# Norms' small steps and half of the state sums on GpSimd, softplus and an attention reciprocal kept in PSUM

## The chip, the cores and the metric

The kernel runs on one core of a Trainium2 chip. The metric is the time of one execution on the device in microseconds (us); lower is better. The core's engines work side by side, each through its own queue in order: PE (TensorE, matmuls), DVE (VectorE), ACT (ScalarE), POOL (GpSimd), and SP, which only issues transfers here. SBUF is the on-chip memory that all of them use; PSUM holds what PE writes, and DVE and ACT read and write it too.

## The reference, cut to what matters

Four sequences of 1024 tokens of 256 values pass four sub-layers, each as x = x + layernorm(f(layernorm(x))):

```python
x = x + _layernorm(_L0_attn_ref(_layernorm(x), ...))  # 4 layers of linear attention and MLP
x = x + _layernorm(_L0_ffn_ref(_layernorm(x), ...))   # a gated low-rank layer
x = x + _layernorm(_L1_attn_ref(_layernorm(x), ...))  # a state space model (SSM)
x = x + _layernorm(_L1_ffn_ref(_layernorm(x), ...))   # 8 experts, one per token, at most 320 each
```

A norm is (x - mean) / sqrt(var + 1e-5). In an attention layer, with q and k passed through elu + 1, the output is divided by a sum:

```python
z = 1.0 / (jnp.einsum('blhd,bhd->blh', qp, ksum) + EPS_ATTN)
return jnp.einsum('blhd,bhmd,blh->blhm', qp, kv, z)
```

In the SSM, delta is a softplus, and 16 states per channel run along the sequence and are summed into the output:

```python
delta = jax.nn.softplus(dt @ W_dt + b_dt)
h = h * exp(delta * A) + (delta * u) * B_t        # for each of 16 states
y = sum over the 16 states of h * C_t
```

All is computed in float32.

## The kernel before, in words

**Blocks and units.** The tokens are worked in 8 blocks of 512 (TB), two per sequence, each as 4 tiles of 128 tokens. A unit is one attention layer of one block; two sequences go through the layers in turns. The loop at the end of `layers` calls the parts of several units in each step, so that one unit's matmuls stand beside another's norms: `a_norm` (L654, first norm), `a_turn`, `a_query`, `a_keys`, `a_sums`, `a_fold`, `b_heads` (L777, the division), `b_out` (L790, output and second norm), `f_up` and `f_down` (the MLP), and after the last layer `c_norm` to `c_norm3` and `c_gate` (the low-rank layer). Between the parts, `pump` draws pieces of the SSM and the experts from a generator, `stream`. For each block it runs `front(j)` (L1045: projections, convolution, softplus), `scan(j)` (L1159: the states), `back(j)` (output projection and norms) and `route(j)` (choice of expert). The experts run beside the last two blocks' scans. So attention and SSM overlap once the first sequence has left the attention layers, and the SSM of the last sequence comes after all of them.

**The order of the work.** No instruction goes out as it is written in the code. `Program.record` (L191) notes each with its operands and with what it will cost by a table of costs, a fixed part and a part per column for each operation of each engine (GPSIMD_NS at L144 is POOL's). `Program.order` (L289) then goes through all of them as a list scheduler. It takes whichever operation can start first by these costs, and gives it a buffer of its pool at that moment. The result is one fixed queue for each engine. So an operation that is cheaper, dearer, or on another engine moves the others too. The profile shows a helper's line, L203, for nearly every operation, so groups are told apart by the names of their tiles.

**A norm.** `ln_stats` (L451) takes mean and variance on DVE (`st`, `mv`). `ln_rsqrt` (L438) takes a first estimate `r` of the reciprocal root on ACT (Ln, then Exp), and improves it in three small DVE operations on 4 columns: `t<-r`, `t<-mv,t` (or `t<-var,t`, `t<-pp,t`), `rs<-t,r`. `norm_on_act` (L470) and `norm_by_act` (L498) then form `nb` on DVE in one more, and ACT applies both to four tiles of 256 columns. 145 norms run: 105 by `norm_on_act`, 32 by `norm_by_act`, and 8 of the experts, which call `ln_rsqrt` alone.

**The division.** In `b_heads`, two 512-column sums per unit are turned into z = exp(-ln(sum + eps)) on ACT, in an SBUF tile of pool `qe`, and DVE multiplies the queries `qT` by it. PE's results go to four PSUM banks of pool `ps_mm` (names `mm`), each given back after its last reader.

**Softplus.** For each of the four 128-channel groups of a block, `front` takes |x| and relu(x) from PSUM on ACT. It forms log(1 + e) of e = exp(-|x|) with a correction (`v1`: one DVE step and two on POOL), adds the relu (`e`, tile `t<-sg,qe` in the profile), multiplies by the input (`t<-xc,t`), and stores both halves of `du` to memory.

**The scan.** A block has 4 groups of 128 channels. Each is worked in 2 rounds r of 4 quarters q, a quarter being 16 channels by 8 states on the 128 partitions, and twice for the two halves of the 16 states (k = 0 and 1): 64 steps a block, 512 in all. Each step is: POOL multiplies `dbu` = (delta u) B, ACT takes `h` = exp(delta A) into PSUM, DVE runs the recurrence over 512 positions in place in `h`, keeps the last column (in a sequence's first half), and multiplies `hc` = h C. PE sums the states of `hc` into `y` by a matmul with a 0/1 matrix; the four quarters of a round go out together. A round's sums are held back and issued during the next one. Buffers: 3 of `dbu`, 2 PSUM banks of `h`, 8 of `hc`, one bank of `y`. The kernel also leaves on POOL the bias additions `X<-X,ro`, scale and residual of other norms (`tok<-tok,...`), a gate product (`ys`), and the scatter transfers of the experts.

Of the kernel before, what the change touches and what calls it, by code (L numbers as in the profile page):

```python
# [9 lines left out]
F32 = mybir.dt.float32  # L10
I32 = mybir.dt.int32
AF = mybir.ActivationFunctionType
# [128 lines left out]
    "reciprocal": (147, 5.84),  # L141
    "memset": (60, 0.83),
}
GPSIMD_NS = {"tensor_tensor": (190, 2.14), "tensor_copy": (200, 0.6), "memset": (100, 0.8)}  # L144
SCALAR_NS = {"activation": (215, 0.85), "copy": (150, 0.85)}

OVERLAP = {"vector": 84, "scalar": 99, "gpsimd": 42}
# [239 lines left out]
def sandwich_kernel(ctx: ExitStack, tc: tile.TileContext, io: dict):  # L387
# [49 lines left out]

    def ln_rsqrt(var, n, scale=1.0):  # L438

        r = small.tile([P, n], F32, tag="r", name="r")  # L440
        nc.scalar.activation(r, var, AF.Ln, bias=eps, scale=scale)
        nc.scalar.activation(r, r, AF.Exp, scale=-0.5)

        t = small.tile([P, n], F32, tag="t", name="t")
        nc.vector.scalar_tensor_tensor(t, r, -0.5 * scale, r, ALU.mult, ALU.mult)
        nc.vector.scalar_tensor_tensor(t, var, LN_EPS / scale, t, ALU.add, ALU.mult)
        rs = small.tile([P, n], F32, tag="rs", name="rs")
        nc.vector.scalar_tensor_tensor(rs, t, 1.5, r, ALU.add, ALU.mult)
        return rs

    def ln_stats(src, n=NT):  # L451
# [18 lines left out]
    def norm_on_act(dst, src):  # L470

        n = src.shape[1]
        mv, rs = ln_stats(src, n)
        nb = small.tile([P, n], F32, tag="nb", name="nb")
        nc.vector.scalar_tensor_tensor(nb, mv[:, :, 0], -1.0, rs, ALU.mult, ALU.mult)
        for i in range(n):
            nc.scalar.activation(
                dst[:, i, :], src[:, i, :], AF.Identity, bias=nb[:, i : i + 1], scale=rs[:, i : i + 1]
            )
# [18 lines left out]
    def norm_by_act(dst, src):  # L498

        sums = small.tile([P, NT], F32, tag="sums", name="sums")  # L500
        for i in range(NT):
            nc.scalar.activation(
                dst[:, i, :], src[:, i, :], AF.Copy, scale=-1.0 / D, accum_out=sums[:, i : i + 1]
            )
        var = small.tile([P, NT], F32, tag="var", name="var")
        for i in range(NT):
            nc.scalar.activation(
                dst[:, i, :],
                src[:, i, :],
                AF.Square,  # L510
                bias=sums[:, i : i + 1],
                accum_out=var[:, i : i + 1],
            )
        rs = ln_rsqrt(var, NT, 1.0 / D)
        nb = small.tile([P, NT], F32, tag="nb", name="nb")
        nc.vector.tensor_tensor(nb, sums, rs, ALU.mult)
        for i in range(NT):
            nc.scalar.activation(
                dst[:, i, :], src[:, i, :], AF.Identity, bias=nb[:, i : i + 1], scale=rs[:, i : i + 1]
            )  # L520
# [23 lines left out]
    def layers(ctx: ExitStack):  # L544
# [232 lines left out]
        def b_heads(u):  # L777
            j = units[u][2]
            qT, den = S[u]["qT"], S[u].pop("den")
            nc.gpsimd.tensor_tensor(X[j], X[j], over_tiles(weight(u)["ro"][:, 0, :]), ALU.add)  # L780
            for c in range(NC_D):
                ps = mm([P, TB], "psa")
                nc.tensor.matmul(ps, den[:, c, :], qT[:, c, :], start=True, stop=True)

                z = apool.tile([P, TB], F32, tag="qe", name="z")
                nc.scalar.activation(z, ps, AF.Ln, bias=attn_eps)
                nc.scalar.activation(z, z, AF.Exp, scale=-1.0)
                nc.vector.tensor_tensor(qT[:, c, :], qT[:, c, :], z, ALU.mult)

        def b_out(u):  # L790
            j = units[u][2]
# [253 lines left out]
        def front(j):  # L1045
# [89 lines left out]
            for db in range(NDB):  # L1135
                ps = mm([P, TB], "psdt")
                o = db * 32
                nc.tensor.matmul(
                    ps, m["w_dt"][o : o + DT_RANK, :], dbc[o : o + DT_RANK, :], start=True, stop=True
                )  # L1140
                bdt = mcol[:, db, M_BDT : M_BDT + 1]
                du = fpool.tile([P, 2, TB], F32, tag="t4", name="du", bufs=3)
                e, lv = du[:, 0, :], du[:, 1, :]
                v1 = fpool.tile([P, TB], F32, tag="sg", name="v1", bufs=2)
                nc.scalar.activation(e, ps, AF.Abs, bias=bdt)
                r = apool.tile([P, TB], F32, tag="qe", name="over")
                nc.scalar.activation(r, ps, AF.Relu, bias=bdt)
                nc.scalar.activation(e, e, AF.Exp, scale=-1.0)
                nc.scalar.activation(lv, e, AF.Ln, bias=1.0)
                nc.vector.tensor_scalar(v1, e, 1.0, -1.0, ALU.add, ALU.add)  # L1150
                nc.gpsimd.tensor_tensor(v1, e, v1, ALU.subtract)
                nc.gpsimd.tensor_tensor(v1, v1, lv, ALU.add)
                nc.vector.tensor_tensor(e, v1, r, ALU.add)
                nc.vector.tensor_tensor(lv, xc[:, db, :], e, ALU.mult)
                store(dud[j][db], du)
                yield 2
                flush()

        def scan(j):  # L1159
# [12 lines left out]
            for db in range(NDB):  # L1172
                y = ps_y.tile([P, TB], F32, tag="y", name="y")

                def sums(tiles, r, k):
                    for q in range(4):
                        nc.tensor.matmul(
                            y[q * 32 : (q + 1) * 32, :],
                            m["gsum"][:, r, :],
                            tiles[q, k],  # L1180
                            start=r == 0 and k == 0,
                            stop=r == GQ - 1 and k == NSH - 1,
                        )

                late = []
                for r in range(GQ):
                    if r == GQ // 2:
                        xl = fpool.tile([P, TB], F32, tag="xl", name="xl")
                        nc.sync.dma_start(xl, xcd[j][db])
                        zl = fpool.tile([P, TB], F32, tag="zl", name="zl")  # L1190
                        nc.sync.dma_start(zl, zsd[j][db])
                    tiles = {}
                    for q in range(4):
                        g = q * GQ + r
                        gg = db * (P // GC) + g
                        dd = []
                        for k in range(2):
                            t = spool.tile([P, TB], F32, tag=f"dd{k}", name=f"dd{k}", bufs=3)
                            nc.sync.dma_start(
                                t,  # L1200
                                dud[j][db][g * GC : (g + 1) * GC, k, :].unsqueeze(1).to_broadcast([GC, SH, TB]),
                            )
                            dd.append(t)
                        for k in range(NSH):
                            dbu = spool.tile([P, TB], F32, tag="dbu", name="dbu", bufs=3)
                            nc.gpsimd.tensor_tensor(dbu, dd[1], Bt[:, k, :], ALU.mult)
                            h = ps_h.tile([P, TB], F32, tag="h", name="h")
                            nc.scalar.activation(
                                h, dd[0], AF.Exp, scale=m["A"][:, gg, k : k + 1]
                            )  # L1210
                            last = m["last_h"][:, gg, k : k + 1]
                            nc.vector.tensor_tensor_scan(
                                h, h, dbu, 0.0 if half == 0 else last, ALU.mult, ALU.add
                            )
                            if half < NB - 1:
                                nc.vector.tensor_copy(last, h[:, TB - 1 : TB])
                            hc = tiles[q, k] = spool.tile([P, TB], F32, tag="hc", name="hc", bufs=8)
                            nc.vector.tensor_tensor(hc, h, Ct[:, k, :], ALU.mult)
                            if late:
                                sums(*late.pop(0))  # L1220
                        yield 4
                    late = [(tiles, r, k) for k in range(NSH)]
                for args in late:
                    sums(*args)
                t = ys[:, db, :]
                nc.vector.scalar_tensor_tensor(
                    t, xl, m["mcol"][:, db, M_D : M_D + 1], y, ALU.mult, ALU.add
                )
                nc.gpsimd.tensor_tensor(t, t, zl, ALU.mult)
                yield 0.8  # L1230
# [586 lines left out]
```

## Time and profile before

| | |
|---|---|
| median of three runs | 2819.7 us (2818.56 to 2821.91) |
| the profiled execution: time, span | 2818.76 us, 2817.0 us |
| PE busy | 2416.0 us (86%), 8628 matmuls |
| DVE busy | 1894.9 us (67%), 3863 instructions |
| ACT busy | 1586.0 us (56%) |
| POOL busy | 1149.9 us (41%), 878 instructions |
| transfers | 342 MB, mean 121 GB/s |
| granted TensorE clock, mean | 0.921 of full speed |

Each float32 matmul shows as two entries. A group's line names the output and input tiles, the shape, the count, then busy us and the mean ns of one, and last the idle time of the engine just before these instructions with what ended it. The largest groups of the engines in question are:

```profile
L203 POOL TENSOR_TENSOR dbu<-dd,bc 128x512 f32<-128x512 f32 x512 | 672.6, 1344 | 479.1 <-DVE h L203 265.5
...
L203 PE MATMUL y<-hc,gsum 128*32 128x512 f32 x1024 | 259.1, 670 | 117.2 <-DVE hc L203 113.2
L203 DVE TENSOR_TENSOR hc<-h,bc 128x512 f32<-128x512 f32 x512 | 342.6, 678 | 16.2 <-PE y L203 14.5
```

So POOL worked 672.6 us on `dbu` in 512 instructions of 1344 ns, and stood idle for 479.1 us before them, mostly until a DVE recurrence (`h`) had ended.

### The profile page before, as it was taken

The page shows a single profiled execution, that of the slowest core. Times are in us where ns is not written, and L with a number is a line of the kernel's source. Part 1 is how long each engine was busy: PE and PEld are TensorE (multiplying, and loading weights), DVE is VectorE, ACT ScalarE, POOL GpSimd, SP SyncE. Part 2 cuts the span into 40 slices and gives each one's busy share as a digit, 9 for nine tenths or more (in the row PEclk, how much of TensorE's full clock was granted, in tenths as well). Part 3 has the DMA queues.
Part 4 walks back from the last instruction along what each step waited for, and adds up shares of the span by engine and source line. Part 5 has one row for each costly group of instructions (what it writes and reads, how often), then busy time and mean ns, then how long its engine had stood idle before and what let it go on. Part 6 is the DMA issues. An engine that isn't in the chain of part 4 may idle for free.

```text
span 2817.0 us, 29326 instructions
## 1 busy us (share of the span) xinstructions
PE 2416.0 (86%) x8628; PEld 1386.3 (49%) x8628; DVE 1894.9 (67%) x3863; ACT 1586.0 (56%) x3277; POOL 1149.9 (41%) x878
## 2 busy tenths in 40 slices
PE   4879799999999999997989998986986975789776
PEld 2546466656555555554645545633543533434343
DVE  3121323244397778886468899997998995699885
ACT  4433554555666666565657756665655544656443
POOL 0100011022154446452135466645654672467663
PEclk8989899999999999998999999997997886899878
DMA  4011110122354353442253454535445343767652
GB/s 116 16 53 48 62 38 25 43 71 79 106 165 131 105 163 130 128 131 81 93 168 123 137 167 154 161 124 172 141 128 158 116 148 124 238 181 212 195 176 49
DMA packets 202214, 342.00 MB, mean 121 GB/s; under 512 B 32197, under 2 KB 79514, under 8 KB 198976
## 3 DMA queue, kind: packets, MB, share of 16 engines
q1 hardware_dynamic: 197760, 334.80, 37.9%
q0 software_dynamic: 4288, 5.27, 1.0%
q8 instruction: 70, 1.15, 0.2%
q14 instruction: 96, 0.79, 0.1%
HBM read 281.13 MB, written 59.92 MB: 121 GB/s over the span
## 4 chain that ended last, share of the span: by engine, by line
DVE 22%; PE 22%; ACT 8%; issue 6%; POOL 4%; DMA 2%; SPq 0%; DVEq 0%; POOLq 0%; ACTq 0%
PE mm L203 18%; DVE h L203 8%; DVE hc L203 4%; ACT tok L203 3%; PE y L203 3%; DVE t L203 2%; POOL dbu L203 2%; DVE st L203 2%; ACT h L203 1%; DVE xc L203 1%; PE kv L203 1%; ACT qe L203 1%; POOL sg L203 1%; DVE kv L203 1%; POOL tok L203 1%
## 5 line engine op out<-in xcount | busy, mean ns | idle before, releaser
L203 POOL TENSOR_TENSOR dbu<-dd,bc 128x512 f32<-128x512 f32 x512 | 672.6, 1344 | 479.1 <-DVE h L203 265.5
L203 ACT ACTIVATE h<-dd,A 128x512 f32<-128x512 f32 x512 | 345.9, 687 | 343.1 <-DVE hc L203 336.1
L203 PE MATMUL mm<-w,fT 128*128 128x256 f32 x2176 | 490.8, 383 | 3.3 <-ACT fT L203 3.2
L203 PEld LDWEIGHTS mm<-w,fT 128*128 128x128 f32 x2176 | 412.7, 191 | 87.0 <-issue 19.3
L203 PE MATMUL y<-hc,gsum 128*32 128x512 f32 x1024 | 259.1, 670 | 117.2 <-DVE hc L203 113.2
L203 DVE TENSOR_TENSOR hc<-h,bc 128x512 f32<-128x512 f32 x512 | 342.6, 678 | 16.2 <-PE y L203 14.5
L203 DVE TENSOR_TENSOR_SCAN h<-h,last_h,dbu 128x512 f32<-128x512 f32 x256 | 322.5, 1278 | 31.4 <-ACT h L203 20.0
L203 DVE TENSOR_TENSOR_SCAN h<-h,dbu 128x512 f32<-128x512 f32 x256 | 306.0, 1218 | 30.3 <-ACT h L203 24.3
L203 POOL TENSOR_TENSOR X<-X,ro 128x1024 f32<-128x1024 f32 x64 | 150.5, 2357 | 396.2 <-ACT tok L203 361.4
L203 PE MATMUL mm<-hT,w1a 128*128 128x512 f32 (+1 forms) x576 | 266.2, 611 | 11.8 <-ACT hT L203 10.6
L203 PE MATMUL mm<-hT,w1b 128*128 128x512 f32 (+1 forms) x576 | 250.2, 584 | 5.0 <-ACT fT L203 3.4
L203 PE MATMUL mm<-wkv,hT 128*128 128x512 f32 x512 | 232.6, 605 | 9.4 <-DVE qT L203 7.6
L203 ACT ACTIVATE fT<-mm,cols 128x512 f32<-128x512 f32 x256 | 170.8, 679 | 66.5 <-PE mm L203 66.3
L203 PE MATMUL mm<-ident,tok 128*128 128x128 f32 x696 | 114.8, 304 | 106.2 <-ACT tok L203 93.7
L203 DVE TENSOR_TENSOR X<-X,mm 128x512 f32<-128x512 f32 x128 | 86.8, 679 | 168.2 <-PE mm L203 167.7
L203 PEld LDWEIGHTS mm<-hT,w1a 128*128 128x128 f32 x576 | 111.3, 202 | 141.1 <-issue 98.4
L203 PEld LDWEIGHTS mm<-hT,w1b 128*128 128x128 f32 x576 | 109.0, 193 | 145.2 <-issue 105.8
L203 PEld LDWEIGHTS mm<-ident,tok 128*128 128x128 f32 x696 | 86.5, 154 | 164.5 <-ACT tok L203 95.6
L203 PEld LDWEIGHTS y<-hc,gsum 128*32 128x32 f32 x1024 | 39.3, 114 | 259.8 <-DVE hc L203 182.7
L203 ACT ACTIVATE tok<-X,nb,rs 128x256 f32<-128x256 f32 x288 | 149.1, 589 | 30.4 <-DVE nb L203 26.8
L203 PEld LDWEIGHTS mm<-wkv,hT 128*128 128x128 f32 x512 | 98.0, 193 | 128.3 <-issue 103.0
L203 ACT ACTIVATE tok<-tok,nb,rs 128x256 f32<-128x256 f32 x252 | 131.5, 589 | 50.0 <-DVE nb L203 45.6
(189 smaller groups left out, 3758.9 us busy)
## 6 DMA issues: line engine op xcount, KB each, us to landing
dd<-dud SPq DMA_DIRECT2D x512, 256.0 KB
w<-in_w_dram SPq DMA_DIRECT2D x16, 1024.0 KB
dud<-t SPq DMA_DIRECT2D x32, 512.0 KB
tok<-in_x_dram SPq DMA_DIRECT2D x16, 512.0 KB
wkv<-in_wkv_dram SPq DMA_DIRECT2D x16, 512.0 KB
w1a<-in_w_dram SPq DMA_DIRECT2D x16, 512.0 KB
w1b<-in_w_dram SPq DMA_DIRECT2D x16, 512.0 KB
t<-in_w_in_dram SPq DMA_DIRECT2D x16, 512.0 KB
```

The source lines that it names most:

```text
L203: getattr(getattr(self.nc, engine), name)(*map(put, args), **{k: put(v) for k, v in kwargs.items()})
```

## The change

Three edits are made together.

1. The small steps of the norms go from DVE to POOL. `ln_rsqrt` forms `ve` = var * scale + eps on POOL, then four POOL steps in place of three on DVE[...]. `nb` takes two POOL steps in `norm_on_act` and one in `norm_by_act`. The table of POOL's costs gains a row for `tensor_scalar`.
2. In blocks 0 to 4 (j < NBLK - 3), POOL adds the two halves of the states of a step pair, `hc` of k = 0 into that of k = 1, and PE sums only the latter.
3. The division and the softplus keep their intermediate values in the PSUM bank that the matmul wrote. In `b_heads`, Ln and Exp work in place there. In the softplus, relu and the sum stay there, and ACT copies the sum to `du`.

```diff
-GPSIMD_NS = {"tensor_tensor": (190, 2.14), ...
+GPSIMD_NS = {"tensor_scalar": (200, 1.1), "tensor_tensor": (190, 2.14), ...
...
     def ln_rsqrt(var, n, scale=1.0):
+        ve = small.tile([P, n], F32, tag="ve", name="ve")
+        nc.gpsimd.tensor_scalar(ve, var, scale, LN_EPS, ALU.mult, ALU.add)
...
-        nc.vector.scalar_tensor_tensor(t, r, -0.5 * scale, r, ALU.mult, ALU.mult)
-        nc.vector.scalar_tensor_tensor(t, var, LN_EPS / scale, t, ALU.add, ALU.mult)
+        nc.gpsimd.tensor_tensor(t, r, r, ALU.mult)
+        nc.gpsimd.tensor_tensor(t, t, ve, ALU.mult)
+        nc.gpsimd.tensor_scalar(t, t, -0.5, 1.5, ALU.mult, ALU.add)
...
-        nc.vector.scalar_tensor_tensor(rs, t, 1.5, r, ALU.add, ALU.mult)
+        nc.gpsimd.tensor_tensor(rs, t, r, ALU.mult)
...
-        nc.vector.scalar_tensor_tensor(nb, mv[:, :, 0], -1.0, rs, ALU.mult, ALU.mult)
+        nc.gpsimd.tensor_scalar(nb, mv[:, :, 0], -1.0, None, ALU.mult)
+        nc.gpsimd.tensor_tensor(nb, nb, rs, ALU.mult)
...
-        nc.vector.tensor_tensor(nb, sums, rs, ALU.mult)
+        nc.gpsimd.tensor_tensor(nb, sums, rs, ALU.mult)
...
-                z = apool.tile([P, TB], F32, tag="qe", name="z")
-                nc.scalar.activation(z, ps, AF.Ln, bias=attn_eps)
-                nc.scalar.activation(z, z, AF.Exp, scale=-1.0)
-                nc.vector.tensor_tensor(qT[:, c, :], qT[:, c, :], z, ALU.mult)
+                nc.scalar.activation(ps, ps, AF.Ln, bias=attn_eps)
+                nc.scalar.activation(ps, ps, AF.Exp, scale=-1.0)
+                nc.vector.tensor_tensor(qT[:, c, :], qT[:, c, :], ps, ALU.mult)
...
-                r = apool.tile([P, TB], F32, tag="qe", name="over")
-                nc.scalar.activation(r, ps, AF.Relu, bias=bdt)
+                nc.scalar.activation(ps, ps, AF.Relu, bias=bdt)
...
-                nc.vector.tensor_tensor(e, v1, r, ALU.add)
-                nc.vector.tensor_tensor(lv, xc[:, db, :], e, ALU.mult)
+                nc.vector.tensor_tensor(ps, v1, ps, ALU.add)
+                nc.scalar.copy(du[:, 0, :], ps)
+                nc.vector.tensor_tensor(du[:, 1, :], xc[:, db, :], ps, ALU.mult)
...
-                            start=r == 0 and k == 0,
+                            start=r == 0 and k == first[r],
...
+                first = [NSH - 1 if j < NBLK - 3 else 0 for r in range(GQ)]
...
+                        if first[r]:
+                            nc.gpsimd.tensor_tensor(hc, tiles[q, 0], hc, ALU.add)
...
-                    late = [(tiles, r, k) for k in range(NSH)]
+                    late = [(tiles, r, k) for k in range(first[r], NSH)]
```

More of the change, by code (lines that the diff above doesn't have):

```diff
@@ L143 @@
 }
-GPSIMD_NS = {"tensor_tensor": (190, 2.14), "tensor_copy": (200, 0.6), "memset": (100, 0.8)}
+GPSIMD_NS = {"tensor_scalar": (200, 1.1), "tensor_tensor": (190, 2.14), "tensor_copy": (200, 0.6), "memset": (100, 0.8)}
 SCALAR_NS = {"activation": (215, 0.85), "copy": (150, 0.85)}
```

## The prediction, made before the changed kernel ran

> **What bounds the kernel now.** I first cut the span into stages, because an 86% busy TensorE averages over stages with different limits. The stage borders come from the rows of the scan's tiles: the first `dbu` starts at 792 us, block 4's last sums are at 2123 us, and from 2310 us on no attention layer is left. The view by stages lists busy us of each engine, then the granted clock and the DMA share:
>
> ```profile
> core 0: us, PE busy (x) PEld busy (x) DVE busy (x) ACT busy (x) POOL busy (x), PEclk, DMA share, GB/s
> 0.00:770.00 770.00, 672.76 (x2335) 419.18 (x2336) 234.29 (x661) 380.91 (x843) 86.09 (x65) 0.94 0.19 59
> 770.00:1260.00 490.00, 464.37 (x1753) 266.62 (x1753) 396.21 (x716) 315.87 (x640) 247.59 (x187) 0.99 0.44 138
> ...
> 1470.00:2150.00 680.00, 594.99 (x2135) 319.97 (x2133) 603.55 (x1113) 429.42 (x831) 376.45 (x287) 0.93 0.47 147
> 2150.00:2310.00 160.00, 129.39 (x470) 74.74 (x470) 151.66 (x283) 78.86 (x145) 103.28 (x77) 0.85 0.44 140
> 2310.00:2450.00 140.00, 92.32 (x292) 49.80 (x292) 81.57 (x235) 74.36 (x158) 49.39 (x43) 0.74 0.52 167
> 2450.00:2817.00 367.00, 282.59 (x983) 140.78 (x982) 311.48 (x518) 182.26 (x399) 224.52 (x174) 0.87 0.57 166
> ```
>
> Call them A (0 to 770), B (770 to 1260), C (1260 to 1470), D (1470 to 2150), E, F and G. A is attention alone, with PE 87% busy. In B blocks 0 and 1 are scanned under the next attention layers: PE 95%, DVE 81%, POOL 51%. In D (blocks 2 to 4) PE is 87.5% and DVE 89% busy, POOL 55%. E and G are DVE's (95% and 85%). F is a serial stretch of norms that end the attention. So what helps is less PE in B, less PE and DVE in D, less DVE in E and G.
>
> Second, the groups of D on DVE, with busy us, mean ns, and the idle time before them:
>
> ```profile
> L203 DVE TENSOR_TENSOR t<-xc,t 128x512 f32<-128x512 f32 x11 | 15.9, 1444 | 0.3
> L203 DVE TENSOR_TENSOR qT<-qT,qe 128x512 f32<-128x512 f32 x15 | 15.4, 1025 | 0.3
> L203 DVE SCALAR_TENSOR_TENSOR t<-r 128x4 f32<-128x4 f32 x30 | 14.9, 497 | 1.3 <-ACT r L203 0.6 <-issue 0.6
> L203 DVE TENSOR_TENSOR t<-sg,qe 128x512 f32<-128x512 f32 x11 | 12.9, 1176 | 8.5 <-POOL sg L203 8.5
> L203 DVE SCALAR_TENSOR_TENSOR t<-mv,t 128x4 f32<-128x4 f32 x23 | 10.4, 454 | 0.2
> ```
>
> The reader is to see two things. A norm's step on four columns takes 450 to 500 ns here, while in A, where POOL does little, the median of the same forms is 161 to 164. And a 512-column product of two SBUF tiles takes 1025 to 1444 ns, where one with an operand in PSUM (`hc`) takes 678.
>
> Third, the waits of D, for what POOL does with its other 45%, and the timeline for how the scan runs at its fastest:
>
> ```profile
> POOL dbu L203 <- DVE h L203: 116.8, 71, 7.2
> ACT h L203 <- DVE hc L203: 105.6, 71, 3.7
> ...
> PE y L203 <- DVE hc L203: 30.8, 14, 14.0
> ```
> ```profile
> 1625.57 2.42 DVE L203 TENSOR_TENSOR_SCAN h<-h,dbu 128x512 f32<-128x512 f32 x2
> ...
> 1629.46 2.42 DVE L203 TENSOR_TENSOR_SCAN h<-h,dbu 128x512 f32<-128x512 f32 x2 [0.17 <-POOL dbu L203]
> ```
> ```profile
> 1626.88 2.50 POOL L203 TENSOR_TENSOR dbu<-dd,bc 128x512 f32<-128x512 f32 x2 [2.75 <-DVE h L203]
> 1630.77 2.51 POOL L203 TENSOR_TENSOR dbu<-dd,bc 128x512 f32<-128x512 f32 x2 [1.39 <-DVE h L203]
> ```
>
> A pair of states takes DVE 3.89 us (1625.57 to 1629.46). POOL works 2.50 of them and has 1.39 left, waiting for a scan to free one of its three `dbu` buffers.
>
> **The change part by part.** Prices: POOL's product takes a median of 1275 ns at 512 columns and 2355 at 1024 (rows of `dbu` and `X`), so 2.11 ns a column and 195 ns fixed. POOL's copy of 4 columns takes 187 to 197. I take 195 ns for each small POOL operation. The ends are 113 ns (its memset of 8 columns) and 331 (the same line drawn through the means, 1344 and 2357).
>
> *Half sums on POOL.* The instruction order of the built kernel has 160 `hc` additions more on POOL and 160 `y` matmuls fewer on PE: 32 in each of blocks 0 to 4. POOL: 160 x 1.275 = 204 us, of which about 78 in B (122 `hc`, 61 additions) and 121 in D (190, 95). PE: the `y` groups are busy 40.2 us in B and 85.5 in D, and half goes: 20 and 43 us. The four quarters of a sum are still issued together. What is queued behind an addition that waits for `hc` is the next `dbu`, and the scan waits for that; the remaining `y` matmuls now wait for POOL instead of DVE, with PE's whole queue behind them. The cover is the 1.39 us gap, in which 1.275 fits, and the third `dbu` buffer. If that cover is gone, each costs the scan up to 1.275 us, 204 us in all; the slower rival below says how much of it shows.
>
> *Norms on POOL.* DVE loses 572 small operations that run: over the 145 norms, 40.1 us for `t<-r`, 44.5 for the second `t`, 37.0 for `rs`, 33.5 for `nb`, together 155 us. Of these 45.7 are in D (14.9+10.4+2.7+7.8+6.2+3.7), 26.5 in A. DVE also no longer stands waiting for `r` (67 us, 51.5 of it in A, where it isn't the limit). POOL gains five per norm and one or two for `nb`: 725 + 242 = 967, x 0.195 = 189 us (109 to 320 by the ends), in D 203 x 0.195 = 40. In latency, DVE's four steps begin 0.2 us apart (7.54, 7.74, 7.94, 8.13), and ScalarE's apply starts 0.8 us after `t`. POOL has five after `r`, at 0.195 plus about 0.06 between dependent ones (`sg<-sg,t`: 1.9 us idle over 32): 1.3 us. So 0.5 us more per norm in an empty queue. In A, 10 times PE's matmuls stood waiting for a norm's `tok` (45.8 us): +5. The other 32 norms of A hide behind matmuls of other units; uncovered, they cost 16 more. C +2, F (9 serial norms) +4. In the scan stages, the order puts `dbu`, additions and the like between `t` and `rs` in 45 of the 145 chains, 100 in all; DVE had 117 of its own there, mostly the shorter `hc`. So I let latency stand even there.
>
> Here two rules of the Trainium skill pull apart. GPSIMD Engine Reference, "4.1 Engine selection", says elementwise work belongs on VectorE, GpSimd being about twice as slow. `dbu` against `hc` agrees (1275 against 679), and doubling 161 ns gives 0.32 us a step: POOL +311 us instead of +189, a count of engine time that speaks against moving. SBUF — State Buffer, "Who interferes with whom", says a VectorE instruction with two SBUF inputs and a GpSimd one that reads SBUF shut each other out for a whole instruction. The rows of D show it: 497 ns against 164. Priced alone, 30 D norms take DVE 30 x 4 x 0.161 = 19 us; by the rows 46. The move takes the 46, so I go by the rows.
>
> *Reciprocal and softplus in PSUM.* Products with one PSUM operand cost 0.68 (`hc`). `qT<-qT,qe`: 54.0 us to 64 x 0.68 = 43.5, so -10.5; softplus's two: 33.8 + 39.1 to 43.5, so -29.4; in D -5 and -14. ACT gains 32 copies of 584 ns = 19 us, hidden in its 44% idle; uncovered they cost 19. The price is in PSUM banks: a softplus now keeps one of the four `mm` banks through Exp, Ln, a DVE step, two POOL steps, the DVE sum and the copy, about 0.63+0.63+0.53+2.55+0.68+0.58 = 5.6 us longer, 32 times. The reciprocal keeps one 1.3 us longer, 64 times. Matmuls fill a bank in about 1.2 us and ACT drains it in 0.68, so three banks suffice: zero, at most one bank's 1.2 us each of 32, 38 us; at best a freed `qe` buffer gives a few us back. I take zero. No DMA is added or moved: SP's queue has as many instructions as before.
>
> **The sum.** D: PE falls from 595 to 552, DVE from 604 to about 539, POOL rises from 376 to 376+121+40 = 537. All three then stand near 80% of 680. The smaller cut, PE's 43, is what can come off; with POOL newly loaded I credit half, -21. What is late next there is POOL's additions. B: PE was the limit, POOL reaches 248+78+30 = 356 of 490, so most of PE's 20: -17. E: 9 norms and little else, -8. G: 15 norms (about 16 us of DVE) and 8 softplus (7), DVE 85% busy, but its norms queue behind scatters of 1.58 us on POOL: -9. A +5, C +2, F +4. Together -44 us. The profiled execution took 2818.76 us (span 2817.0), the median is 2819.7; both give about 2775.
>
> **Rivals.**
> *Slower: POOL's queue becomes the limit of B and D.* It runs in order, and its idle time in D, 304 us, is made of waits for particular scans. If a share s can't be filled, D lasts 537 + 304s. It decides from s = 0.47, where D is 680 again. At s = 0.6, D is 719 (+39), B 356 + 0.6 x 242 = 501 (+11), the rest -6: 2862. For it: at full scan rate 2.50 + 1.275 = 3.78 of 3.89 us are POOL's, and `X`, `tok` and `sg` work of 1.3 to 2.4 us falls between. Against it: the scan runs at that rate only part of D (190 states in 680 us, 3.6 us each, against 1.95).
> *Latency shows: norms wait in POOL's queue.* All 42 of A exposed (+16) and half of 29 us of longer chains in the scan stages (100 x 1.3 against 101 us of DVE's): 2775 + 31 = 2806. For it: PE's waits for `tok`. Against it: most norms are planned well ahead.
> *Full gain.* PE's 43 and 20 come off whole, E and G give 32: 11 - 95 = -84, 2735. For it: the lock waits that end in D. Against it: POOL.
> *Washed out*, between the second and the first: about 2820.
>
> **How the numbers follow.** Chances: about 2775 0.45, full gain 0.14, latency 0.06, washed out 0.06, slower 0.29. A measurement of this kernel tells about 0.2% (5.6 us) from no change. Faster 0.65, same 0.06, slower 0.29. The likeliest case alone spans 2750 to 2795. The range, 2728 to 2880, takes in the full gain and the slower case up to s = 0.63 (D +49, B +19, the rest -6: 2880), and leaves out about 0.15.
>
> **What would show it.** In the changed profile: POOL near 1.15+0.20+0.19 = 1.54 ms busy, small steps near 195 ns; DVE near 1.70 ms; `y` groups 704 entries (1024 less 320), about 195 us; D shorter, with `qT` and softplus products at 0.68 us. Wrong if scans wait for `dbu` by far more than the present 13.4 us, if PE's wait for `y` grows past its 113, or if A lengthens by more than 10 us.

## The result and the profile after

The changed kernel takes 2794.14 us (median of four runs, 2787.44 to 2799.51), the kernel before 2820.8 beside it: 0.9906 of its time, 95% interval 0.989 to 0.9922. That is 27 us less. The profiled execution is the shortest of the four, 2787.44 us with a span of 2785.7, 31.3 us under the span of before.

The stages of the changed kernel, in the same view and columns as before (the last row ends with the new span):

```profile
0.00:770.00 770.00, 658.40 (x2286) 411.15 (x2287) 206.61 (x487) 371.45 (x827) 137.55 (x336) 0.93 0.19 58
770.00:1260.00 490.00, 461.74 (x1659) 269.89 (x1658) 383.31 (x640) 325.04 (x659) 360.11 (x409) 0.99 0.44 139
...
1470.00:2150.00 680.00, 588.03 (x1982) 324.23 (x1981) 575.01 (x1005) 438.85 (x853) 541.82 (x595) 0.92 0.48 152
...
2450.00:2786.00 336.00, 269.22 (x955) 136.60 (x953) 279.94 (x449) 174.56 (x388) 229.49 (x250) 0.88 0.58 171
```

In the first row PE does fewer matmuls than before (2286 entries against 2335): stage A has become longer. In D, POOL is 80% busy, as forecast, and DVE fell from 604 to 575. PE fell only from 595 to 588, although the 384 `y` entries of this stage have become 194. The groups of the page say the same of the whole span:

```profile
L203 POOL TENSOR_TENSOR dbu<-dd,bc 128x512 f32<-128x512 f32 x512 | 663.0, 1333 | 147.8 <-DVE h L203 104.5
...
L203 PE MATMUL y<-hc,gsum 128*32 128x512 f32 x704 | 222.2, 664 | 84.0 <-DVE hc L203 57.6
...
L203 POOL TENSOR_TENSOR hc<-hc,hc 128x512 f32<-128x512 f32 x160 | 213.8, 1336 | 52.6 <-DVE hc L203 46.8
```

POOL's idle time before `dbu` fell from 479 to 148 us: the new work fills it. But `y` lost 31% of its entries and only 14% of its busy time (259.1 to 222.2). The waits of D show what took the place of the old ones:

```profile
POOL dbu L203 <- DVE h L203: 31.7, 29, 4.1
...
PE y L203 <- POOL hc L203: 19.4, 11, 6.5
...
DVE h L203 <- POOL dbu L203: 16.2, 13, 2.7
```

POOL waits 32 us for scans, not 117; PE waits 19 us for POOL's sums. Scans wait for `dbu` for 28.5 us in the whole span, against 13.4 before. The products in D cost what an operand in PSUM promised (they were 1025 to 1444 ns):

```profile
L203 DVE TENSOR_TENSOR qT<-qT,mm 128x512 f32<-128x512 f32 x16 | 10.8, 678 | 3.1 <-ACT mm L203 3.1
...
L203 DVE TENSOR_TENSOR mm<-sg,mm 128x512 f32<-128x512 f32 x12 | 8.3, 690 | 1.8 <-POOL sg L203 1.8
L203 DVE TENSOR_TENSOR t<-xc,mm 128x512 f32<-128x512 f32 x12 | 8.3, 688 | 6.2 <-ACT t L203 5.9
```

To say where the time went, I cut each trace at the start of three of the sixteen `kvo<-mm` copies on ACT (one for each sequence and attention layer, made once the sums of both its units are there): the 7th (737.0 us before), the 12th (1406) and the 16th (2148). The predicted terms are those of the forecast.

| us | to the 7th (A) | to the 12th (B, C) | to the 16th (D) | to the end (E, F, G) | span |
|---|---|---|---|---|---|
| before | 737.0 | 669.2 | 741.4 | 669.4 | 2817.0 |
| predicted | +5 | -15 | -21 | -13 | -44 |
| after | +15.0 | -12.0 | -19.2 | -15.1 | -31.3 |

The profiled execution is 12.7 us short of the forecast -44; 10.0 of these are A's. The other stages came out close to their sums. Whether the reasons were right is another question, which the table can't answer.

### The profile page after: what moved, and what is told of

The parts are those of the page before. It is cut to its first block, busy times and chain, and to the rows that moved or that the text cites. A ratio compares the mean times of both kernels' runs of the same rounds, so it can differ in the third digit from the quotient of the medians.

```text
span 2785.7 us, 29116 instructions
## 1 busy us (share of the span) xinstructions
PE 2378.6 (85%) x8308; PEld 1380.3 (50%) x8308; DVE 1752.6 (63%) x3291; ACT 1591.2 (57%) x3309; POOL 1527.6 (55%) x2005
## 4 chain that ended last, share of the span: by engine, by line
PE 41%; DVE 20%; POOL 14%; ACT 14%; issue 8%; DMA 3%; SPq 0%; POOLq 0%; DVEq 0%; ACTq 0%
PE mm L203 36%; DVE h L203 7%; ACT tok L203 6%; POOL dbu L203 5%; DVE hc L203 3%; PE kv L203 2%; PE y L203 2%; POOL tok L203 2%; POOL hc L203 2%; DVE st L203 2%; DVE xc L203 2%; POOL t L203 2%; ACT h L203 2%; DVE kv L203 1%; ACT t L203 1%
## 5 line engine op out<-in xcount | busy, mean ns | idle before, releaser
L203 POOL TENSOR_TENSOR dbu<-dd,bc 128x512 f32<-128x512 f32 x512 | 663.0, 1333 | 147.8 <-DVE h L203 104.5
L203 PE MATMUL y<-hc,gsum 128*32 128x512 f32 x704 | 222.2, 664 | 84.0 <-DVE hc L203 57.6
L203 POOL TENSOR_TENSOR hc<-hc,hc 128x512 f32<-128x512 f32 x160 | 213.8, 1336 | 52.6 <-DVE hc L203 46.8
L203 ACT ACTIVATE fT<-mm,cols 128x512 f32<-128x512 f32 x256 | 170.8, 682 | 85.5 <-PE mm L203 84.8
L203 POOL TENSOR_SCALAR ve<-mv 128x4 f32<-128x4 f32 (+1 forms) x105 | 20.7, 197 | 335.1 <-DVE mv L203 323.0
```

The source lines that it names most:

```text
L203: getattr(getattr(self.nc, engine), name)(*map(put, args), **{k: put(v) for k, v in kwargs.items()})
```

## The experiments

Each version is timed against the kernel before, run beside it; differences are between these medians. A stage's time comes from one profiled execution each, and the executions of one kernel differ by up to 15 us, so small differences between stages are weak. Theory 1 was the prediction's: each edit gives what its terms say, so the three add up. The rival: the edits act through one another (POOL's reads, PE's queue), so that one alone can cost and the three together gain.

**Each edit alone.** The first takes all of edit 1, with its row of the cost table, and nothing else; its diff against the kernel before begins:

```diff
-        nc.vector.scalar_tensor_tensor(t, r, -0.5 * scale, r, ALU.mult, ALU.mult)
+        nc.gpsimd.tensor_tensor(t, r, r, ALU.mult)
...
```

> The norms' small steps on GpSimd, and nothing else of the change. My theory: the first 770 us lose about 12 us, since each exposed norm ends 0.55 us later and nothing there gains from a freer VectorE; later about 46 us of VectorE's work and its waits for GpSimd go from blocks 2 to 4, worth about 20 us. Sum: about 2810 (-10). Rival, lock: VectorE's lock waits were the real limit of the scan stages, then 2790 or less. Rival, queue: norms stuck in GpSimd's queue cost more than they free, then over 2825.

Measured: 2830.6 us, 1.0037 (1.0024 to 1.0051). Slower by 10, where a gain of 10 was expected; A alone is 13.3 us longer (750.3 against 737.0).

All of edit 2, the half sums, and nothing else, from the kernel before:

```diff
+                        if first[r]:
+                            nc.gpsimd.tensor_tensor(hc, tiles[q, 0], hc, ALU.add)
...
```

> Only the half sums of blocks 0 to 4 on GpSimd. The trace of the changed kernel shows less TensorE time saved than forecast (y groups 222 us busy instead of 195), since sums go out one or two at a time instead of four to eight. My theory: about 2808 (-12), mostly in the stage of blocks 0 and 1. Rival, co-bound: without the norm edit VectorE still limits blocks 2 to 4 and the gain is under 6 us (2815 or more). Rival, GpSimd: slower than 2825, with recurrences waiting for dbu.

Measured: 2843.08 us, 1.0068 (1.0054 to 1.0082). Slower by 23: the edit on which the forecast put most of its gain is by itself the costliest. It is as slow as the GpSimd rival said, but recurrences wait for `dbu` only 23.1 us in all (13.4 before), so not by that rival's reason.

All of edit 3, the PSUM edits, and nothing else:

```diff
+                nc.scalar.activation(ps, ps, AF.Exp, scale=-1.0)
...
+                nc.scalar.activation(ps, ps, AF.Relu, bias=bdt)
...
```

> Only the reciprocal and the softplus kept in PSUM. My theory: VectorE is relieved by 40 us of which half lies in stages that it limits, so about 2812 (-8). Rival, banks: holding one of four banks longer stops TensorE, then 2825 or more, with the first 770 us longer (no softplus is there, but 64 reciprocals are).

Measured: 2803.84 us, 0.9943 (0.9929 to 0.9956). Faster by 17. The three alone add to +16, together they give -27. Theory 1 falls here.

**Stage A.** The changed kernel, but norms recorded before the first scan keep their three steps and `nb` on DVE. The flag is set at the start of `scan`:

```diff
+    nc.scanning = False
...
     def ln_rsqrt(var, n, scale=1.0):
+        if not nc.scanning:
+            r = small.tile([P, n], F32, tag="r", name="r")
...
+            return rs
...
             begun.append(j)
+            nc.scanning = True
```

> The changed kernel, but norms recorded before the first scan keep their small steps on VectorE in three operations. If the longer chain of small steps is what made the attention-only stage 15 us longer (8th kvo copy at 752 us instead of 737), that copy is back at 737 to 741 and the total is about 2782 (-12 against the changed kernel). If held PSUM banks or the new order did it, the copy stays near 752 and the total near 2794.

Measured: 2782.38 us, 0.9869 (0.9854 to 0.9884), 12 us under the changed kernel, and the copy meant there (the 7th) came at 735 us, against 752. So A's cost is the chain on an otherwise idle POOL. Most of the -12 us of B and C goes with it: with early norms on DVE the stretch from the 7th to the 12th copy takes 667.9 us, 1.3 less than before and not 12. So what A loses is in part won back there. The timeline of the kernel before, then of the changed kernel, shows such a chain:

```profile
83.76 0.16 DVE L203 SCALAR_TENSOR_TENSOR t<-r 128x4 f32<-128x4 f32 x1 [0.60 <-ACT r L203]
...
84.61 1.58 ACT L203 ACTIVATE tok<-X,nb,rs 128x256 f32<-128x256 f32 x3 [0.88 <-DVE nb L203]
```
```profile
88.11 0.20 POOL L203 TENSOR_TENSOR t<-r 128x4 f32<-128x4 f32 x1
88.39 0.20 POOL L203 TENSOR_TENSOR t<-t,ve 128x4 f32<-128x4 f32 x1
88.68 0.19 POOL L203 TENSOR_SCALAR t<-t 128x4 f32<-128x4 f32 x1
88.95 0.20 POOL L203 TENSOR_TENSOR rs<-t,r 128x4 f32<-128x4 f32 x1
89.23 0.20 POOL L203 TENSOR_TENSOR nb<-nb,rs 128x4 f32<-128x4 f32 x1
89.46 1.58 ACT L203 ACTIVATE tok<-X,nb,rs 128x256 f32<-128x256 f32 x3 [1.43 <-POOL nb L203]
```

Five dependent steps start 0.28 us apart: 1.35 us from the first to ACT's start, where DVE's four took 0.85. Over the 41 norms ahead of 737 us, ACT starts to apply a norm 1.62 us (mean) after `r` is ready, against 1.27 before. That is 0.35 us for each and 14 us for all 41, worked out from the timelines: if nearly all of it showed, it makes A's +15. PE pays for it, by the waits of the first 770 us, of the kernel before, the changed kernel and this experiment:

```profile
PE mm L203 <- ACT tok L203: 45.8, 10, 17.5
```
```profile
PE mm L203 <- ACT tok L203: 59.1, 8, 18.8
```
```profile
PE mm L203 <- ACT tok L203: 43.3, 9, 17.5
```

**Leaving one out.** The changed kernel without the half sums (`first` left out, both halves summed by PE):

> Norms on GpSimd and the PSUM edits, without the half sums. Alone, the three edits gave +10, +23 and -17 us, which adds to +16, where together they give -27. If the edits simply added, this is about 2813. If the half sums pay only once VectorE is relieved of the norms (theory: they load GpSimd, whose reads of SBUF shut VectorE's two-input steps out, and with the norms gone few such steps are left), this is slower than the changed kernel, 2805 to 2815. Rival: the half sums cost here as they cost alone, then this is about 2772.

Measured: 2801.55 us, 0.9933 (0.992 to 0.9946). Then the same with the early norms on DVE, as above:

> As the run before it, but with the norms ahead of the first scan kept on VectorE. By the first run of that kind it should be 12 us below the run without half sums: about 2800 by the theory that half sums pay in the combination, about 2760 by the rival.

Measured: 2789.02 us, 0.9889 (0.9875 to 0.9904). In both cases the half sums are worth 7 us (2801.55 - 2794.14, 2789.02 - 2782.38; in each pair the two intervals just meet), where the forecast gave their PE time 38. Also, the DVE norms in A are worth 12.5 us here too.

Without the PSUM edits (z and relu back in their `qe` tiles):

> Norms and half sums on GpSimd, with reciprocal and softplus as before. If edits added: 2853. If norms and half sums help each other (fewer two-input steps left on VectorE for GpSimd's reads to lock out), clearly less: 2808 to 2815, that is the changed kernel plus the 17 us that the PSUM edits gave alone.

Measured: 2834.31 us, 1.0045 (1.0031 to 1.006). Without edit 1 (norms on DVE):

> Half sums and PSUM edits, with the norms' small steps on VectorE as before. If edits added: 2826. If the half sums need the norms off VectorE, it stays there, 2820 to 2830, with blocks 3 and 4 ending late as in the run with half sums alone. Rival: it is the PSUM edits that the half sums need (VectorE's products of two SBUF tiles gone), then 2785 to 2800.

Measured: 2815.7 us, 0.9979 (0.997 to 0.9988). Both of these fall between what their two theories expected. The eight combinations, in us against the kernel before:

| | no half sums | half sums |
|---|---|---|
| neither | 0 | +23 |
| norms | +10 | +13 |
| PSUM | -17 | -5 |
| norms and PSUM | -19 | -27 |

The PSUM edits gain wherever they are added: 17 alone, 28 beside half sums, 30 beside norms, 40 beside both (from the unrounded medians, as in the next sentence). The half sums cost 23 or 11 where DVE keeps the small norm steps, cost 3 without them, and gain only when both other edits are there.

By the cuts of above, the half sums alone cost 17.0 of their 24.5 us of span in D (758.4 against 741.4). With the norms moved they cost nothing there (733.6 against 734.9), and with both other edits they gain 7 (722.2 against 729.1). The row of D for the half sums alone:

```profile
1470.00:2150.00 680.00, 580.35 (x1926) 319.07 (x1926) 612.20 (x1106) 417.77 (x812) 494.76 (x376) 0.91 0.45 142
```

DVE has got busier (612 against 604 us) though its own work is the same, and it did less of it in those 680 us (1106 instructions against 1113). The steps that got longer read two SBUF tiles (`xc`, here of the kernel before and then with half sums); those with one operand in PSUM (`hc`) took 678 ns before and take 678 still:

```profile
L203 DVE SCALAR_TENSOR_TENSOR xc<-xi,mcol,xc 128x512 f32<-128x512 f32 x96 | 81.1, 845 | 39.2 <-ACT xc L203 31.4 <-ACT xi L203 4.8 <-ACT r L203 2.3
```
```profile
L203 DVE SCALAR_TENSOR_TENSOR xc<-xi,mcol,xc 128x512 f32<-128x512 f32 x96 | 89.7, 934 | 33.9 <-ACT xc L203 26.7 <-ACT xi L203 4.7 <-ACT r L203 1.6
L203 DVE TENSOR_TENSOR hc<-h,bc 128x512 f32<-128x512 f32 x512 | 342.8, 678 | 8.4 <-PE y L203 5.6 <-POOL hc L203 1.2
```

In the whole span, DVE instructions took 292 us beyond the shortest one of their own tiles and form, summed over all, against 255 before (worked out from the trace). The half sums add 38 us of this excess alone, 56 with the PSUM edits, 31 with the norms and 28 with both. The other edits take away steps that are hit: without half sums, the excess is 197 with PSUM alone, 191 with norms alone, and 138 with both. But what the half sums add doesn't follow what they cost: it is largest beside the PSUM edits, where they cost 11 us and not 23. So it is shown that DVE's steps get longer; how much of the run's time this makes is not.

**The two PSUM edits apart.** Softplus alone, with its sum, copy and product as in the change:

```diff
-                nc.scalar.activation(r, ps, AF.Relu, bias=bdt)
+                nc.scalar.activation(ps, ps, AF.Relu, bias=bdt)
...
```

> Only the softplus kept in PSUM, on the kernel before. Both PSUM edits together gave -17 us. Theory, path: the softplus stands in the chain that opens each block's scan, and its two products took 1.06 and 1.22 us behind GpSimd's reads instead of 0.68; so it carries most, -11 to -17 (2804 to 2810). Rival: the reciprocal carries it, then this is within 4 us of before.

Measured: 2811.0 us, 0.9972 (0.9962 to 0.9982), just above the expected 2804 to 2810. The division alone, with Ln and Exp in place:

```diff
-                nc.vector.tensor_tensor(qT[:, c, :], qT[:, c, :], z, ALU.mult)
+                nc.vector.tensor_tensor(qT[:, c, :], qT[:, c, :], ps, ALU.mult)
...
```

> Only the reciprocal kept in PSUM, on the kernel before. It saves 10 us of VectorE over 64 products and some 3 us of ScalarE, beside other work: by the path theory 0 to -5 (2816 to 2821), first kvo copies up to 1 us earlier. By the rival -11 to -17.

Measured: 2824.26 us, 1.0011 (1.0003 to 1.0018). Softplus gives 10 of the 17 us, the division by itself loses 3 (0 to -5 was expected), and the two together gain 10 more than their sum. Both free `qe` buffers, and the list scheduler reorders every queue for each; which of these joins them was not settled.

**The four sums side by side.** In PE's queue of the changed kernel, the 160 `y` matmuls of blocks 0 to 4 stand in 81 groups: 39 of one, 20 of two, 7 of three and 15 of four. In the kernel before, 320 stood in 82 groups, 17 of them of eight. The description's "the four quarters of a round go out together" holds for the code and not for the queue: the scheduler sends each as soon as its `hc` is there. This experiment takes the kernel with early norms on DVE, and records the four as one operation:

```diff
-                    for q in range(4):
-                        nc.tensor.matmul(
-                            y[q * 32 : (q + 1) * 32, :],
...
+                    outs = [y[q * 32 : (q + 1) * 32, :] for q in range(4)]
+                    ins = [m["gsum"][:, r, :]] + [tiles[q, k] for q in range(4)]
...
+                        for q in range(4):
+                            nc.nc.tensor.matmul(
...
+                    nc.add("tensor", emit, outs, ins, 4 * busy, 5 * busy + 190)
```

> The changed kernel with early norms on VectorE (2782 measured), in which the four quarters' sum matmuls are planned as one piece, so that they stand next to each other in TensorE's queue; in the changed kernel 59 of 81 runs of them in blocks 0 to 4 are of one or two. Theory: that is where the forecast 63 us of TensorE time went (37 measured), so the y groups fall from about 225 to about 200 us busy or less and the total to 2770 to 2778. Rival: TensorE's time there is off the path, or waiting for the fourth addition stops the queue, then 2780 to 2795.

Measured: 2775.78 us, 0.9847 (0.9834 to 0.986): the fastest version, 6.6 us under the same kernel with loose sums (their intervals just overlap), 18 under the changed kernel. All 40 groups of blocks 0 to 4 are now of four. The page:

```profile
L1204 PE MATMUL y<-hc,gsum 128*32 128x512 f32 x704 | 131.4, 685 | 38.7 <-DVE hc L203 24.9
```

Each entry still lasts about 0.68 us, but four run at once, so the group is busy 131 us instead of 225 in the same kernel with loose sums. PE timelines show it: in the changed kernel, then in the next experiment.

```profile
1497.85 1.04 PE L203 MATMUL y<-hc,gsum 128*32 128x512 f32 x2
1502.48 1.05 PE L203 MATMUL y<-hc,gsum 128*32 128x512 f32 x2
```
```profile
1602.45 1.07 PE L1183 MATMUL y<-hc,gsum 128*32 128x512 f32 x8
```

A lone matmul (two entries) holds PE for 1.04 us, four neighbours (eight entries) for 1.07.

**Are lone sums what made the half sums costly?** The half sums alone on the kernel before, with the four as one operation by the edit just shown:

> The half sums alone (edit 2 on the kernel before), with the four sums of a round recorded as one operation, so that they stand side by side in PE's queue. The half sums alone took 2843, 22 us more than the kernel before, with y busy 228.5 us. Theory 1, lone matmuls: the loss is PE's, because the halved y matmuls go out one by one and each holds PE for its full time; then y falls to about 130 us as in the changed kernel with four sums, PE loses some 95 us, and most of the 22 comes back: 2826 or less. Theory 2, POOL: the loss is the 160 additions on POOL, which take turns with DVE's steps on two SBUF tiles and stand ahead of dbu; grouping then gives what it gave in the whole change, 7 us or less: 2836 or more, with DVE still near 1929 us busy and the scan's waits for dbu near the 23 us of the half sums alone. Between 2826 and 2836 both have a part.

Measured: 2829.54 us, 1.0035 (1.0021 to 1.0048): between the two. Of the 23 us, 11 are left, so the lone matmuls have a part. The rest stays, and in D nearly all of it: 754.7 us between the 12th and 16th copies, against 758.4 with loose sums and 741.4 before. The row of D:

```profile
1470.00:2150.00 680.00, 556.23 (x1937) 319.70 (x1935) 610.71 (x1105) 422.21 (x819) 494.54 (x378) 0.90 0.45 143
```

PE is down to 82% and POOL at 73%, while DVE stays 90% busy at 611 us. Freeing 24 us of PE hardly shortened this stage. So what the half sums still cost there is likely to lie with DVE and POOL, of which DVE is the fuller; no run shows this by itself.

## Why the prediction was right or wrong

The direction and the range were right, and the forecast of 2775 was 19 us too low. Three steps of the reasoning failed, and the total came as near as it did partly by luck.

**The half sums' PE time, 20 us in B and 43 in D: wrong.** The step that failed is "The four quarters of a sum are still issued together". The `y` entries of blocks 0 to 4 were busy 127.6 us before and still took 99.1 of 322 entries after. In B the group fell from 40.2 to 29.3, 11 us and not 20, and in D from 85.5 to 68.8, 17 us and not 43. Grouping them by hand brought the first figure to 51.2 (320 entries, half sums alone) and showed the mechanism. That B with C and D still came out near the forecast, -12 and -19, is luck: without the half sums the changed kernel already has -10 and -12 there. The prediction credited these stages to the wrong edit, and most of the -12 of B and C goes with A's delay: with early norms on DVE it is -1.3.

**What limits D: partly wrong.** It took PE's cut as "what can come off". The half sums alone lengthen D by 17 us with less PE work, and their grouping doesn't mend that. That points to DVE, which stays 90% busy in both and whose two-SBUF steps get longer beside POOL's new reads; that DVE sets D's length is argued and not shown. The lock was priced as a gain of moving the norms, but not as a cost of 160 more additions on POOL. The sizes forecast for D were POOL 537 (measured 542), DVE about 539 (575), PE 552 (588).

**The latency of A: right mechanism, wrong size.** +5 was forecast for A, +15.0 came. The 0.5 us per norm was about right (1.35 against 0.85 in the chain shown, 0.35 on average). The term that failed is "10 times" 0.5: it counted the waits of PE that the trace of before shows, and took the other 32 norms as hidden. 41 norms at 0.35 us make 14. "If A lengthens by more than 10 us" was named as a sign against it.

**What held.** The 967 small POOL steps take 210 ns on average and 203 us in all (195 and 189 forecast), POOL is 1527.6 us busy (1.54 ms), the products 678 to 690 ns (0.68). The PSUM banks showed no price: with PSUM edits alone A is 2.8 us shorter. E to G gave -15.1, with -13 forecast. DVE fell to 1752.6 us and not 1.70 ms: `kv<-kv,tok` went from 1293 to 1618 ns (+10 us), `sg<-t` from 526 to 762 (+8), `xc<-xi,mcol,xc` from 845 to 896 (+5), all beside the fuller POOL.

**The rivals.** The slower case has the half sums alone to speak for it (+23) and norms with half sums (+13), but not by the mechanism given: POOL's queue filled (its wait for scans in D fell to 32 us). That case took all of POOL's 304 us of idle time in D as waits for particular scans, but only 117 of them were. And scans waited for `dbu` only 28.5 us in all. As to norms that wait in POOL's queue: they cost A, where the queue is empty, by their latency alone.

**What stays open.** Why the division and the softplus gain more together than apart; why the norms, which take 114 us off DVE alone (1894.9 to 1780.5), gain next to nothing outside A by themselves (2080.0 us from the 7th copy to the end before, 2078.5 with norms alone), and gain 21 us in all beside both others, A's loss included. That each version is a new schedule of all five queues is a reason to expect such remainders, and shows none of them.

## What to carry to other kernels

Price a move to another engine on the engine that limits the stage, with what the mover's reads do to that engine's steps: here the same 160 additions cost 23 us or gained 7, by which other edits stood beside them. Narrow matmuls are cheap only as neighbours, so look at the queue, and not at the loop, before counting their time. And where an engine has nothing else to do, a longer chain of small steps shows in full: keep it on the engine with the shortest chain there.

## What the runs showed of the hardware

PE's clock answers to its own gaps, and this can take back a part of what PE is spared. Stretches of 4 us of D in the kernel with half sums alone, with PE busy, granted clock and DMA:

```profile
2016.00:2020.00 4.00, 4.00 (x24) 1.00 0.02 9
2020.00:2024.00 4.00, 1.21 (x4) 1.00 0.48 144
2024.00:2028.00 4.00, 3.93 (x24) 0.67 0.61 207
2028.00:2032.00 4.00, 2.84 (x4) 0.50 0.32 108
```

The timeline of the same kernel:

```profile
2024.07 0.39 PE L203 MATMUL mm<-w_gate,t 128*128 128x8 f32 x2 [2.86 <-ACT t L203]
...
2031.19 1.92 PE L203 MATMUL y<-hc,gsum 128*32 128x512 f32 x2 [1.16 <-POOL hc L203]
2035.06 1.92 PE L203 MATMUL y<-hc,gsum 128*32 128x512 f32 x2 [1.95 <-POOL hc L203]
```

PE has no work for 2.86 us, and at 2025.4 us, 1.3 us after it has work again, the clock goes to half. A lone `y` then takes 1.92 us instead of 1.04, between new waits for POOL's sums. Over this whole trace, of 48 gaps of 2 us or more that began at full clock, 45 were followed by half clock within 3.4 us of their end, but only 6 of 62 gaps of 0.3 to 1 us. The clock was at half for 516 us in all, against 447 in the kernel before. The Trainium skill, "TensorE: Matmul & The Clock Gate", "Part 1: The HAM clock gate", says that an idle window of about 3.4 us halves the clock and a busy one restores it. These rows show it more easily set off than that: the gap is shorter than 3.4 us, and PE was busy for 39% of the 3.4 us before the fall.

The half sums lowered the mean granted clock of all executions in each of five pairs: 0.910 against 0.919 alone, 0.914 against 0.919 with norms, 0.912 against 0.922 with PSUM, 0.915 against 0.922 with both, and 0.918 against 0.924 with early norms on DVE. Grouping lowered it again, 0.910 to 0.904 and 0.918 to 0.908. Between executions of one kernel, 0.01 of clock goes with about 12 us (167 executions of 14 kernels, each against its own kernel's mean). By that estimate, 6 to 11 us of what the half sums could give, and 7 to 12 of what the grouping could, went into the clock. This is a correlation; no run changed the clock alone.
